# A quantized block of a convolution chain: its depthwise filters on row and column parities in four column strips, with a three-part bfloat16 input

## The chip, the cores and the metric

The kernel runs on one core of a Trainium2 chip. The metric is the device time of one execution in microseconds (us), lower is better; the shown time is the median of three runs. One more execution was profiled: every time below that isn't a run's time comes from its page or its trace.

## The reference, cut to what matters

Four layers follow one another on a tensor of 32 images, 96 channels, 56 x 56. Before each of layers 0, 1, 2 and 3 stands a group norm over groups of three channels of one image, and each layer's result is added to its input. Layer 0 is an inverted bottleneck with squeeze and excite (1x1 to 576 channels, 3x3 depthwise, 1x1 back to 96), layer 1 a three-level wavelet convolution, layer 3 a 9 x 9 depthwise diffusion filter. The change is in layer 2, again an inverted bottleneck, with weights and activations quantized to 4 bits:

```
def quant_w(w, bits):
    t = jnp.tanh(w)
    t = t / (2.0 * jnp.max(jnp.abs(t))) + 0.5
    return 2.0 * quantize_k(t, bits) - 1.0
def act_q(x, bits):
    x = jnp.clip(x, 0.0, 1.0)
    return quantize_k(x, bits)
...
1x1 conv 96 -> 576 (quant_w), bias, batch norm, act_q
3x3 depthwise on 576 (quant_w), bias, batch norm, act_q
1x1 conv 576 -> 96 (quant_w), bias, batch norm
```

The quantized values are integers (weights odd numbers up to 15, activations 0 to 15 after scaling), so bfloat16 holds them exactly. The normalized image is not: it has to go into the first product in more than one part.

## The kernel before, in words

The layers run one after another; between them the tensor goes through device memory (y0, y1, y2). Layers 0 and 2 keep channels on partitions and run over the 32 images; layers 1 and 3 keep rows on partitions and run over channels. An image in layer 2 lies in SBUF as 224 x 14 values: rows in four tiles of 14, columns split by their remainder modulo 4, two images interleaved in a pair (`xt`, three pairs of buffers).

Layer 2 is `layer2` (L987 on), with constants made by `Layer2` (L887 on). Those are prepared in stages beside layer 1's work (`prepare`, L973): tanh, the largest value, quantizing, batch norm factors, and the diagonal matrices of the depthwise filters (`diagonals`, L946: 45 products of 128 x 64). The steps of an image have letters, and `L2_ORDER` (L68) is the order in which every engine issues them: `run_steps` walks the list once for each image n from -2 to 33, a step with "-" belonging to image n-1, "--" to n-2, "+" to n+1. TensorE, VectorE and ScalarE follow this order as written; transfers are issued by SP, powers by GpSimd.

The steps:

- s, u, v, b, x: statistics by `channel_stats` (L91), group mean and variance by small matmuls (L1045, L1053), factors, and the mean taken off the image (L1066).
- h, l: the image times 1/deviation rounded to float32r (`high`, ScalarE, L1079), and what that leaves over (`low`, VectorE, L1085), both written in natural column order, so every fourth element.
- e: `expand` (L1099). Five blocks of 128 channels (the last holds 64 channels twice), four row tiles each: 80 float32r matmuls of 96 x 128 by 392 columns (L1107), a high and a low one into the same PSUM. Each tile is evicted with batch norm and rounding to int16 (`evict`, L1092: ScalarE at L1097, or VectorE at L1095 for those in `L2_ON_DVE`).
- m: `activate`, the clip to 0..15 into a padded bfloat16 tile of pitch 57 (L1116).
- a: `depthwise` (L1129). Nine taps, each a 64 x 64 diagonal matrix; four of them lie side by side in the array (`quarter`, L1121, matmuls at L1126): 648 matmuls of 64 x 64 by 392 columns for an image. A call of a full block fills two PSUM tiles, a call of the half block one; 18 tiles are evicted for an image.
- n: `activate2`, the clip of those (L1116).
- j, d: `project` (L1158), 40 matmuls of 128 x 96 by 392 (L1163), and `add` (L1166), which scales the result and adds it to the image (L1170). In between, r (L1090) has made the image its own residual.
- o: `store` (L1175): statistics for layer 3's norm; after every second image the pair is stored to y2 by six transfers, and the pair's buffer refilled from y1 by six more (`fetch`, L1010).

PSUM has one pool of four tiles of two banks, which all steps share. Layer 0 already does its filters in another way (`filtered`, L417 to L436, and `project`, L474 to L492): in float32, on planes of row and column parities, in strips of 32 array columns. In the trace a float32 matmul is two records.

Of the kernel before, what the change touches and what calls it, by code (L numbers as in the profile page):

```python
# [10 lines left out]
F32 = mybir.dt.float32  # L11
# [26 lines left out]
NM = 12  # L38
MAGIC = 12582912.0
# [29 lines left out]
    e00 e10 e11 e12 l3 j0- d0- e01 e20 e02 e21 r u+ e03 e13 j1- m0 e22 d1- e30 m1 e40 v+ j2- d2- e31  # L69
    e41 e23 b+ e42 j3- x+ e32 e33 m2 d3- m3 s++ e43 h0+ m4 a00 a10 o- a11 n1 a01 a20 h1+ a30 a21 l0+  # L70
    a31 n0 a40 l1+ n2 l2+ a41 n3 n4
"""
L2_ON_DVE = {"e00", "e20", "a301", "a201"}
# [21 lines left out]
def store_norm(tc, S, pool, psum, mv, dram, bias, room=None):  # L95
# [8 lines left out]
    ps = psum.tile([128, 2, 512], F32, tag="mm", name="pn")  # L104
# [79 lines left out]
def layer0(ctx, tc, S, x, w, y0, norm1, tables, aside):  # L184
# [21 lines left out]
    GC = 32  # L206
# [680 lines left out]
class Layer2:  # L887


    def __init__(self, ctx, tc, S, w, y1):  # L890
# [6 lines left out]
        CC, HALF, N9 = NBLK - 1, 64, 2 * NBLK - 1  # L897
        def tile(name, shape, dtype=F32):
            return cp.tile(shape, dtype, tag=name, name=name)

        w1, w2, w3 = (tile(f"{n}q", shape, dtype) for n, shape, dtype in (
            ("l2_w1", [C, NBLK * 128], F32R), ("l2_w2", [128, NBLK, 9], F32), ("l2_w3", [128, N9 + 1, C], BF16)))
        eye2, diag = tile("eye2", [128, HALF]), tile("diag2", [128, NBLK, 9, HALF], BF16)
        mid, out5 = tile("mid2", [128, 10, N9]), tile("out5", [C, 5, 1])
        s1, o1, s2, o2 = (tile(n, [128, N9]) for n in ("s1", "o1", "s2", "o2"))
        s3, o3 = (tile(n, [C, 1]) for n in ("s3", "o3"))
        self.constants = w1, w3, diag, s1, o1, s2, o2, s3, o3

        raw, at = [], 0
        for name, o in (("l2_w1", w1), ("l2_w2", w2), ("l2_w3", w3)):
            p, n = o.shape[0], math.prod(o.shape[1:])
            t = self.pairs[1].rearrange("p r i q -> p (r i q)")[:p, at : at + n]
            m, a = (tile(f"{name}{x}", [p, 1]) for x in "ma")
            raw.append((name, t, o if len(o.shape) == 2 else o.rearrange("p a b -> p (a b)"), m, a))
            at += n

        def load():  # L920
            for name, t, *_ in raw:
                v = w[name]
                nc.sync.dma_start(t, v if len(v.shape) == 2 else v.rearrange("p a b -> p (a b)"))

            nc.sync.dma_start(mid, w["l2_mid"])
            nc.sync.dma_start(eye2, w["eye2"])
            nc.sync.dma_start(out5, w["l2_out"])

        def largest():
            for _, t, _, m, a in raw:  # L930
# [4 lines left out]
        def quantized():  # L935
            for _, t, o, _, a in raw:
# [6 lines left out]
            nc.vector.memset(w3[HALF:, N9 - 1, :], 0.0)  # L943
            nc.vector.memset(w3[:HALF, N9, :], 0.0)

        def diagonals(k):  # L946
            for t in range(9):
                nc.vector.tensor_scalar(diag[:, k, t, :], eye2, w2[:, k, t : t + 1], None, ALU.mult)

        norms = ((mid[:, 0:5, :], s1, o1, 1.0 / 15.0, 15.0), (mid[:, 5:10, :], s2, o2, 1.0 / 225.0, 15.0),  # L950
# [36 lines left out]
def layer2(ctx, tc, S, k2, y1, y2, norm3):  # L987
# [11 lines left out]
    pool = ctx.enter_context(tc.tile_pool(name="l2", bufs=1))  # L999
    sm = ctx.enter_context(tc.tile_pool(name="l2s", bufs=3))  # L1000
    up = ctx.enter_context(tc.tile_pool(name="l2u", bufs=3))
    ap = ctx.enter_context(tc.tile_pool(name="l2a", bufs=6))
    psum = ctx.enter_context(tc.tile_pool(name="l2p", bufs=4, space=PSUM))
    CC, HALF, N9 = NBLK - 1, 64, 2 * NBLK - 1
    w1, w3, diag, s1, o1, s2, o2, s3, o3 = k2.constants
# [17 lines left out]
    apad = padded(cp, nc, NBLK, BF16, "apad")  # L1023
    mv_all = cp.tile([C, B, 2], F32, tag="mv2", name="mv2")
    ims = {}

    def image(b):

        if b not in ims:
            pair, xt = xs.pop(b)  # L1030
            ims[b] = {"b": b, "pair": pair, "xt": xt, "a2": [None] * NBLK, "u": [None] * NBLK, "ps": [None] * NP}
        return ims[b]

# [8 lines left out]
    def group_mean(im):  # L1042
        mean, var = im["mv"][:, 0:1], im["mv"][:, 1:2]
        ps = psum.tile([128, 2, 512], F32, tag="mm", name="pn")
# [6 lines left out]
    def group_variance(im):  # L1051
        ps = psum.tile([128, 2, 512], F32, tag="mm", name="pv")
# [15 lines left out]
    def natural(t, p):  # L1068

        return t.rearrange("c (t r) (q p) -> c p t r q", t=NP, p=NPH)[:, p]  # L1070

    def phase(im, p):
        return im["xt"].rearrange("c (t p r) q -> c p t r q", t=NP, p=NPH)[:, p]

    def high(im, half):
        if half == 0:
            im["hi"] = pool.tile([C, H, W], F32R, tag="hi", name="hi")
        for p in (2 * half, 2 * half + 1):
            nc.scalar.activation(natural(im["hi"], p), phase(im, p), AF.Copy, scale=im["rstd"])  # L1079

    def low(im, i):
        if i == 0:
            im["lo"] = pool.tile([C, H, W], F32R, tag="lo", name="lo")
        for p in range(NPH):
            nc.vector.scalar_tensor_tensor(natural(im["lo"], p)[:, i], phase(im, p)[:, i], im["rstd"],  # L1085
                                           natural(im["hi"], p)[:, i], ALU.mult, ALU.subtract)
# [5 lines left out]
    def evict(out, ps, s, o, c, on_dve):  # L1092

        if on_dve:
# [4 lines left out]
    def expand(im, k, i):  # L1099

        if i == 0:
            im["u"][k] = up.tile([128, HW], I16, tag="u", name="u")
        ps = psum.tile([128, 2, 512], F32, tag="mm", name="ps")
# [390 lines left out]
```

## Time and profile before

| what | time |
|---|---|
| median of 3 runs | 5833.67 us (5833.61 to 5834.31) |
| the profiled execution's own time | 5845.79 us |
| its span in the trace | 5844.0 us |
| layer 2, first statistics to last addition | 3606.6 to 5376.6 us |
| first and last group norm of layer 2 (L1057) | 3612.8 and 5276.1 us |
| first and last expansion matmul (L1107) | 3621.8 and 5337.5 us |
| layer 3, first matmul | 5422.5 us |
| layer 2 from 3622 to 5376 (1754 us): TensorE busy | 1624.0 us |
| VectorE busy in that window | 1208.5 us |
| ScalarE busy in that window | 1212.2 us |
| granted TensorE clock over the span | 0.98 |

A line of a group gives the line of code, the engine, the operation, what it writes and reads, the shape and the count; then busy time and the mean duration of one in ns; then the idle time of the engine before such instructions, and what ended it. "issue" there means that the engine waited for nothing that the profile shows. PEld is TensorE's weight load, which runs beside matmuls. Matmul durations are latencies: successive ones overlap, so a matmul's cost is the distance between starts. A line of the timeline gives start, length, engine, code line, operation and how many were merged. A line of the windows table gives busy time and count for PE, PEld, VectorE, ScalarE and GpSimd, then clock, DMA share and GB/s.

### The profile page before, as it was taken

What the parts mean: (1) busy time and instruction counts of PE and PEld (TensorE: products, weight loads), DVE (VectorE), ACT (ScalarE), POOL (GpSimd) and SP (SyncE); (2) the same over time, 40 slices, a digit from 0 to 9 for tenths busy, and PEclk for the clock granted to TensorE, in tenths of its full rate; (3) what the DMA queues carried; (4) which work ended last, traced back from release to release, by engine and by line L of the source; (5) the groups of instructions that cost most, each with busy time, mean ns of one, the idle gap of its engine ahead of it and who ended that gap; (6) DMA issues with size and microseconds to landing.
All of it is one profiled execution on the core that took longest, in us unless ns stands there. A gap on an engine that the chain in (4) does not pass through costs nothing.

```text
span 5844.0 us, 137224 instructions
## 1 busy us (share of the span) xinstructions
PE 5504.4 (94%) x59688; PEld 3074.4 (53%) x59688; DVE 4693.6 (80%) x5388; ACT 4182.6 (72%) x6036; POOL 240.1 (4%) x156
## 2 busy tenths in 40 slices
PE   5999999999999999995999997999899999897899
PEld 2333333333333333333566665777777777775444
DVE  6999999999999999994766665766667667665777
ACT  5888888888888888874565564766667677675555
POOL 5000000000000000000000000000000000000000
PEclk9999999999999999997999999999999999999999
DMA  3122333332222222235576668386796796754888
GB/s 98 18 56 56 62 60 57 58 58 54 56 49 48 55 52 56 46 26 89 144 141 147 154 147 89 26 44 42 49 46 37 51 49 40 50 31 34 234 253 245
DMA packets 1306412, 454.32 MB, mean 78 GB/s; under 512 B 1123841, under 2 KB 1301753, under 8 KB 1303889
## 3 DMA queue, kind: packets, MB, share of 16 engines
q1 hardware_dynamic: 1305809, 445.54, 50.3%
q8 instruction: 468, 7.67, 0.6%
q14 instruction: 135, 1.11, 0.1%
HBM read 284.44 MB, written 214.08 MB: 85 GB/s over the span
## 4 chain that ended last, share of the span: by engine, by line
PE 83%; ACT 6%; issue 4%; DVE 3%; DMA 2%; POOL 1%; SPq 1%; POOLq 0%; ACTq 0%; DVEq 0%
PE psd L432 17%; PE psd L1126 11%; PE psj L483 10%; PE ps L365 7%; PE pc L842 7%; PE ps L1107 7%; PE pse L388 6%; PE pc L1280 6%; PE psj L1163 3%; ACT hi L1079 2%; PE pc L826 2%; ACT a L1097 2%; PE pa L800 2%; PE pc L816 1%; ACT u L1097 1%
## 5 line engine op out<-in xcount | busy, mean ns | idle before, releaser
L406 DVE SCALAR_TENSOR_TENSOR h<-hpad,l_wdw,h 128x3136 f32<-128x3136 f32 x512 | 1782.2, 3481 | 9.1
L432 PE MATMUL psd<-plane,filt 128*32 128x392 f32 (+5 forms) x16384 | 1084.3, 485 | 0.0
L1126 PE MATMUL psd<-apad,diag 64*64 64x392 bf16 x20736 | 935.9, 333 | 128.1 <-issue 73.0
L1126 PEld LDWEIGHTS <-diag 64*64 64x64 bf16 x20736 | 705.0, 107 | 354.9 <-issue 184.8
L432 PEld LDWEIGHTS psd<-plane,filt 128*32 128x32 f32 (+1 forms) x16384 | 390.1, 108 | 675.2 <-issue 622.7
L1097 ACT ACTIVATE a<-psd,o,s 128x784 int16<-128x784 f32 x448 | 424.1, 999 | 347.8 <-PE psd L1126 347.7
L672 ACT COPY T<-raw 32x112 f32<-32x112 f32 (+2 forms) x1440 | 462.6, 384 | 267.6 <-DMA raw<-tdiff 219.9
L1097 ACT ACTIVATE u<-ps,o,s 128x784 int16<-128x784 f32 x576 | 536.9, 1003 | 160.2 <-PE ps L1107 141.8
L365 PE MATMUL ps<-xn,l_wboth 96*128 96x392 f32 (+1 forms) x1536 | 465.4, 505 | 23.9 <-ACT xn L347 23.0
L406 DVE SCALAR_TENSOR_TENSOR hc<-hhalf,l_wdw,hc 128x1568 f32<-128x1568 f32 x256 | 473.8, 1851 | 16.1 <-ACT hc L399 9.4
L1107 PE MATMUL ps<-hi,l_w1q 96*128 96x392 f32 x1280 | 461.7, 361 | 9.2 <-ACT hi L1079 9.2
L1280 PE MATMUL pc<-x,T 128*112 128x416 f32 (+1 forms) x1152 | 416.2, 524 | 40.3 <-DMA raw<-tdiff 39.6
L842 PE MATMUL pc<-x,T 128*112 128x416 f32 (+1 forms) x1152 | 445.9, 523 | 0.0
L1107 PE MATMUL ps<-lo,l_w1q 96*128 96x392 f32 x1280 | 437.3, 342 | 0.2 <-issue 0.2
L388 PE MATMUL pse<-xn,l_wboth 96*32 96x392 f32 x4096 | 391.2, 500 | 3.2 <-ACT hab L409 3.2
L365 PEld LDWEIGHTS ps<-xn,l_wboth 96*128 96x128 f32 (+1 forms) x1536 | 219.2, 173 | 248.8 <-issue 56.5
L1280 PEld LDWEIGHTS pc<-x,T 128*112 128x112 f32 x1152 | 204.8, 178 | 251.2 <-issue 233.3
L409 ACT ACTIVATE hab<-psd,o,s 128x784 f32<-128x784 f32 x256 | 284.1, 1114 | 58.6 <-PE psd L432 55.8
L375 ACT ACTIVATE hpad<-ps,o,s 128x784 f32<-128x784 f32 x256 | 278.4, 1104 | 49.2 <-PE ps L365 47.9
L483 PE MATMUL psj<-h,wg 128*32 128x392 f32 x3072 | 307.0, 514 | 1.4 <-DVE wg L472 1.4
L483 PE MATMUL psj<-hab,wg 128*32 128x392 f32 x3072 | 304.3, 510 | 0.0
L392 ACT ACTIVATE plane<-pse,o,s 128x784 f32<-128x784 f32 x256 | 256.2, 1001 | 24.9 <-PE pse L388 19.8
(234 smaller groups left out, 7608.2 us busy)
## 6 DMA issues: line engine op xcount, KB each, us to landing
X<-y SPq DMA_DIRECT2D x192, 392.0 KB
y<-xt SPq DMA_DIRECT2D x180, 392.0 KB
xt<-in_x_dram SPq DMA_DIRECT2D x16, 2352.0 KB
y<-y SPq DMA_DIRECT2D x96, 392.0 KB
xt<-y SPq DMA_DIRECT2D x96, 392.0 KB
out_dram<-y SPq DMA_DIRECT2D x96, 392.0 KB
twav<-zwav SPq DMA_DIRECT2D x768, 36.8 KB
raw<-twav SPq DMA_DIRECT2D x96, 168.0 KB
```

What stands on the lines that cost most here:

```text
L365: nc.tensor.matmul(ps[p, j, :NT], wexp[:, k * 128 : k * 128 + 128][:, m], im["xn"][:, j, rows, :].rearrange("c h w -> c (h w)"), start=Tru ...
L388: nc.tensor.matmul(ps[f * GC : (f + 1) * GC, half, :NT].rearrange("p (r w) -> p r w", w=W2), wexp[:, c : c + GC], im["xn"][:, f % 2, r0 : ...
L406: nc.vector.scalar_tensor_tensor(h2, taken(im, k, t), wdw[:, k, t : t + 1], h2, ALU.mult, ALU.add)
L409: nc.scalar.activation(view, ps, AF.Silu, bias=bi[1][:, c : c + 1], scale=sc[1][:, c : c + 1], accum_out=accum)
L432: nc.tensor.matmul(ps[at * GC : (at + 1) * GC, r, :NT].rearrange("p (r w) -> p r w", w=W2)[:, r0 - half * n : r1 - half * n, q0:q1], filt[ ...
L483: nc.tensor.matmul(ps[s * GC : (s + 1) * GC, t, :NT].rearrange("c (m r q) -> c r q m", m=2, q=W4), wg[p, k, c * GC : (c + 1) * GC], phases ...
L672: nc.scalar.copy(to.rearrange("x t (p s) -> x t p s", p=NPH), v[:, k])
L842: nc.tensor.matmul(ps[:PH, to], st["T"][j][:, h, k, :], st["x"][:, j, h, of], start=False, stop=(n == NK - 1))
L1097: nc.scalar.activation(out, ps, AF.Identity, bias=o[:, c : c + 1], scale=s[:, c : c + 1])
L1107: nc.tensor.matmul(ps[:, j, :NT], w1[:, k * 128 : k * 128 + 128], im[part][:, r0 : r0 + RT, :].rearrange("c h w -> c (h w)"), start=(part ...
L1126: nc.tensor.matmul(ps[q, j, :NT].rearrange("p (r w) -> p r w", w=W), diag[p, k, t, :], v, start=(t == 0), stop=(t == 8))
L1280: nc.tensor.matmul(ps[:, :, to], st["T"][:, h, k, :], st["x"][:, h, :, of], start=(n == 0), stop=(n == NK - 1))
```

## The change

In layer 2 alone:

- The image goes into the first product in three bfloat16 parts: `high` rounds to bfloat16 (ScalarE), `remainder` (y) takes the rest in float32 (VectorE), `middle` (i) rounds that (ScalarE), `low` (l) rounds what is left (VectorE). All stay in the image's own layout.
- `expand` works on groups of 32 channels (18 of them): for each group, three parts, two row parities and four strips of 32 array columns, one for each parity of row and column, 24 bfloat16 matmuls. The result lies as four parity planes on four sets of 32 partitions.
- `depthwise` filters these planes with 32-column matrices that gather several taps: a call has 32 matmuls, in four full-height rounds of four and two rounds of eight half-height ones; 18 calls for an image. Border taps shorten the column range, and there is no padding. The filter matrices are made from `l2_wphase` by five products.
- `project` runs in strips of 32 columns (40 matmuls a call, three calls); it puts the columns back in the image's order as it writes PSUM. `add` has four pieces a call.
- All evictions are on ScalarE (`L2_ON_DVE` is empty). PSUM is four named tiles, taken in turn (`bank`). Planes and filtered tiles are fixed sets of buffers (five and six).
- `L2_ORDER` is new; an image now ends ("o") two images behind.

The diff, cut to its core:

```diff
-    e00 e10 e11 e12 l3 j0- d0- e01 e20 e02 e21 r u+ e03 e13 j1- m0 e22 d1- e30 m1 e40 v+ j2- d2- e31
-    e41 e23 b+ e42 j3- x+ e32 e33 m2 d3- m3 s++ e43 h0+ m4 a00 a10 o- a11 n1 a01 a20 h1+ a30 a21 l0+
-    a31 n0 a40 l1+ n2 l2+ a41 n3 n4
+    n4-- s m3-- m4- n0-- a21-- e21- e00- u e32- e02- n2-- a32-- a33-- e01- e13- v e23- a31-- a30-- e30-
+    e22- n1-- n3-- e11- e20- e03- e12- j2-- e33- r- x m2- e31- m1- h j0-- d2-- a40- m0- d0-- a11- y a03-
+    a41- i j1-- d1-- b a23- a20- a00- a10- a22- l a01- a12- e41 e40 o-- a02- e10 a13-
...
-L2_ON_DVE = {"e00", "e20", "a301", "a201"}
+L2_PLANES, L2_ACTS = 5, 6
+L2_ON_DVE = set()
...
         def diagonals(k):
-            for t in range(9):
-                nc.vector.tensor_scalar(diag[:, k, t, :], eye2, w2[:, k, t : t + 1], None, ALU.mult)
+            n = slice(4 * k * NM, min(4 * (k + 1), NGR) * NM)
+            shape = [128, n.stop - n.start, GC]
+            nc.vector.tensor_tensor(filt[:, n, :], eye4.unsqueeze(1).to_broadcast(shape),
+                                    taps[:, n].unsqueeze(2).to_broadcast(shape), ALU.mult)
...
+    def bank(name):
+
+        turn[0] += 1
+        n = turn[0] % 4
+        return psum.tile([128, 2, 512], F32, tag=f"mm{n}", name=name)
...
+    def high(im):
+        nc.scalar.activation(hi, im["xt"], AF.Copy, scale=im["rstd"])
+
+    def remainder(im):
+        nc.vector.scalar_tensor_tensor(rest, im["xt"], im["rstd"], hi, ALU.mult, ALU.subtract)
+
+    def middle(im):
+        nc.scalar.copy(mid, rest)
+
+    def low(im):
+        nc.vector.tensor_tensor(lo, rest, mid, ALU.subtract)
...
+    def expand(im, k, g):
+
+        ps, n = bank("ps"), QUAD * k + g
+        for part in (hi, mid, lo):
+            v = part.rearrange("c (t p r a) q -> c p a t r q", t=NP, p=NPH, a=2)
+            for j in range(2):
+                for f in range(4):
+                    nc.tensor.matmul(
+                        ps[f * GC : (f + 1) * GC, j, :NT].rearrange("p (t r q) -> p t r q", t=NP, q=W4),
+                        w1[:, n * GC : (n + 1) * GC], v[:, f % 2 + 2 * j, f // 2],
+                        start=(part is hi), stop=(part is lo),
+                    )
+        evict(plane(im, k)[:, g, :].bitcast(I16).rearrange("p (m q j) -> p j m q", q=W4, j=2),
+              ps[:, :, :NT].rearrange("p j (m q) -> p j m q", q=W4), s1, o1, n, f"e{k}{g}")
...
+        rounds = [[(r, 2 * r + p, every, 0, 0)] for r in range(2)] + [[(r, 4 + 2 * r + p, every, 0, q)] for r in range(2)]
+        rounds += [[(0, n, bottom, -1, dq), (1, n, top, 1, dq)] for n, dq in ((8 + p, 0), (10 + p, q))]
+        n = HH // 2
+        for x, products in enumerate(rounds):
+            for at, (g, part) in enumerate(parts):
+                for r, m, rows, dm, dq in products:
+                    r0, r1 = max(part * n, -dm), min((part + 1) * n, HH - dm)
+                    q0, q1 = max(0, -dq), W2 - max(0, dq)
+                    nc.tensor.matmul(
+                        ps[at * GC : (at + 1) * GC, r, :NT].rearrange("p (r w) -> p r w", w=W2)[
+                            :, r0 - part * n : r1 - part * n, q0:q1],
+                        filt[rows, (QUAD * k + g) * NM + m, :], planes[rows, g, r0 + dm : r1 + dm, q0 + dq : q1 + dq],
+                        start=(x < 2), stop=(x == len(rounds) - 1),
+                    )
...
+        for t in range(2):
+            for k in range(CC):
+                for s in range(LAST + 1):
+                    strip(s, t, k, slice(128), t * HH, start=(k == 0), stop=False)
+        for s in range(LAST + 1):
+            for t in range(2):
+                strip(s, t, CC, slice(t * HALF, (t + 1) * HALF), 0, start=False, stop=True)
```

In `strip`, the output is written as `ps[...].rearrange("c (m r q) -> c r q m", m=2, q=W4)`, a scatter within PSUM.

## The prediction

> **What bounds the kernel now.** I read the page's busy table and its DMA queues, then the groups by line between 3630 and 5376 us (Layer 2, the only layer whose work the diff changes), then TensorE's weight loads in order of time, then a table of windows over two images.
>
> ```profile
> PE 5504.4 (94%) x59688; PEld 3074.4 (53%) x59688; DVE 4693.6 (80%) x5388; ACT 4182.6 (72%) x6036; POOL 240.1 (4%) x156
> ...
> q8 instruction: 468, 7.67, 0.6%
> ```
>
> Every matmul is a pair of records, a weight load and a matmul. Queue 8 brings instructions: 7.67 MB in 468 packets is 16.4 KB each, and 119,968 TensorE records (592 semaphore ones among them) over 468 is 256. So all of queue 8 is TensorE's program, 256 instructions (64 B each) at a time.
>
> ```profile
> L1126 PE MATMUL psd<-apad,diag 64*64 64x392 bf16 x20736 | 935.9, 333 | 128.1 <-issue 73.0 <-ACT a L1097 52.1 <-ACT u L1097 0.5
> L1107 PE MATMUL ps<-hi,l_w1q 96*128 96x392 f32 x1264 | 454.8, 360 | 0.0
> L1097 ACT ACTIVATE a<-psd,o,s 128x784 int16<-128x784 f32 x448 | 424.1, 999 | 347.8 <-PE psd L1126 347.7
> L1163 PE MATMUL psj<-a,l_w3q 128*96 128x392 bf16 x1024 | 212.1, 329 | 0.0
> ```
>
> TensorE leads: ScalarE waits for it. Its means are latencies; the cost is the distance between starts. In the timeline, L1107 matmuls begin every 0.177 us (4401.65, 4401.83), L1163 every 0.1665, and L1126 runs 288 loads in 12.15 us, 42.2 ns each, 169 ns for four that run side by side. Per image: 80 x 0.1775 = 14.2 us expand, 162 x 0.169 = 27.4 us filter, 40 x 0.1665 = 6.7 us project, 0.5 us statistics: 48.8 us. The first and last group norm lie at 3612.8 and 5276.1: 31 intervals of 53.65 us. Some 4.9 us an image are stalls. Which?
>
> ```profile
> 5293.49 5.25 PEld L1126 LDWEIGHTS <-diag 64*64 64x64 bf16 x128 [2.08 <-issue]
> 5299.70 5.22 PEld L1126 LDWEIGHTS <-diag 64*64 64x64 bf16 x128 [0.96 <-issue]
> 5306.19 5.25 PEld L1126 LDWEIGHTS <-diag 64*64 64x64 bf16 x128 [1.26 <-issue]
> 5312.40 3.70 PEld L1126 LDWEIGHTS <-diag 64*64 64x64 bf16 x92 [0.96 <-issue]
> ```
>
> Bursts of exactly 128 loads, one 256-instruction packet, then a wait for nothing that the profile names. Queue 8's packets start at 5291.03, 5297.31, 5303.73 and 5309.94, always 2.4 to 2.5 us before a burst begins. TensorE is **waiting for its own instructions**. In Layer 2, 59 gaps of over 0.4 us fall on such a border, 92.8 us in all (2.9 us an image); the rest is filter groups waiting for ScalarE to clear PSUM. [...] the packets that were late took a mean 6.39 us while stores run (50 of them), 6.43 while loads run (29) and 3.89 with DMA quiet (13).
>
> ```profile
> 4380.00:4410.00 30.00, 30.00 (x352) 26.63 (x345) 25.17 (x41) 20.70 (x22) 0.55 (x1) 0.99 0.01 2
> 4410.00:4450.00 40.00, 35.75 (x688) 28.51 (x687) 26.66 (x47) 26.87 (x26) 0.00 (x0) 1.00 0.51 59
> 4450.00:4490.00 40.00, 35.80 (x502) 29.92 (x504) 24.73 (x42) 26.34 (x27) 0.54 (x1) 0.96 1.60 65
> ```
>
> The last two columns are the DMA share and GB/s: of each pair of images 30 us are quiet, 40 are stores, 40 are loads. Counted from packets in 1 us steps, 1156 of the 1754 us from 3622 to 5376 have DMA running.
>
> [...] inside Layer 0's L432 the change from 128 to 64 rows takes 411 ns where 309 is usual, so 0.1 us. [...] ScalarE's 784 elements take 1004 ns dense (L392), 1202 at 8 bytes (L347, rows of 14), 1726 at 16 (L1079). [...] L483, which scatters into PSUM, starts a group of four strips every 345 ns, L388 every 330.
>
> **The change, part by part, for one image.**
> *Expand*: three bf16 parts in strips, 18 x 24 = 432 matmuls, 108 groups of four. L388 starts four strips at 7 ns and the next four after 330, the array time of one float32 record; bf16 halves it: 108 x 0.168 = 18.1 us, against 14.2.
> *Filters*: 18 calls of 32 matmuls. L432 does a call (64 records in float32) in 4.19 us (1222.29 to 1226.48). [...] 18 x 1.29 = 23.2 us, against 27.4. [...]
> *Project*: 27 groups at 0.172[...]: 3 x 1.75 = 5.3 us, against 6.7. It scatters into PSUM: bounded by nothing and by a doubling[...]; I take the float32 surplus.
> Sum with statistics: **47.1 us of array, against 48.8**.
> *Instructions*: 432 + 576 + 120 + 4 = 1132 pairs, against 772 (24,704 over 32 in the windows table): 2264 instructions, **8.84 packets where there were 6.03**. At 47.1 us that is 5.33 us a packet, as dense as the bursts above, now all the time.
> *ScalarE*: 36 evictions, back to back 0.92 (1.90 for two, 2.80 for three), 33.1 us[...]. High part and middle part, 3136 elements each, at L399's 2.91: 39 us, from 38. *VectorE*: statistics 8.4, small 1, centre 1.85, remainder 3.5 (L406's 3136), low 3.4, residual 1.9, clips 8.8, twelve adds at 0.58 (L1170) 7.0: 36 us, from 38. Both under TensorE. I let their waits take 5%: 5.6 us a packet.
> *PSUM in turn*: still four tiles of two banks; a filter call takes one, not two. *Border memsets*: 15 on GpSimd, idle for 788 us before; nothing. *Constants*: 45 products of 247 ns become five of some 1.7 (1536 elements at L472's 652 ns for 480, the fixed part taken as 160), and two small loads more, all under Layer 1's matmuls; nothing, and without that cover -2.5 us.
> *Order*: store and refill move from one image behind to two. Both queue on SP as before: 12 transfers for two images, 78 us. From there to the next use by "s" are two iterations, 107 us: covered. The chain "x h y i l" ahead of "e41" is 1.85 + 3 + 3.5 + 2.9 + 3.4 = 15 us; behind "x" stand nine filter calls, three projections and two expansions, some 19 us: covered by 4.
>
> **The sum.** First expand: 3613.4 (the first group norm done) plus that chain, 3628.7, against 3621.8, +7. Packets: 32 x 8.84 = 283. While DMA runs (1156 - 7 = 1149 us; the bytes are the same) a packet takes 6.5, the mean above with a little for unequal latencies: 177. The other 106 at 5.6: 594 us. Draining the last image, whose last filters, clips and projections have no other image beside them: 15. Last matmul at 3628.7 + 1149 + 594 + 15 = 5387, against 5375: +12. Then two more adds, and stores that begin only after the last add (before, from 5371.7 on): +8. Together **+20 us** on the profiled 5845.8 us (span 5844.0), which lies 12 over the median; on the median, **5854**.
>
> **Rivals.**
> *The fetch doesn't bind.* If packets come ahead when the demand is steady, all 283 cost 5.6: 1585 + 15, last matmul at 5229, and 5834 - 146 + 8, **5696**, faster. For it: it needs only a landing within 5.6 us, and quiet stretches show 3.9. Against: 79 late packets under DMA, mean 6.4. Halfway, at 5.9 under DMA: 195 packets and 88 x 5.6, last matmul at 5286, -89 + 8, **5753**. The sign turns near 6.37.
> *PSUM scatter.* If projection doubles, 4.4 us an image: 6.1 us a packet in quiet, and I take half in the rest (6.7): 171 and 112, 1149 + 683 + 15, last matmul at 5476, +101 + 8, **5943**. [...] against: 15 ns in float32.
> *ScalarE binds.* Evictions at L375's 1.10 give 46 us, just under TensorE; quiet packets at 5.9: +32 more, **5886**.
>
> **Chances.** Forecast 0.45 (slower 0.30, same 0.10, faster 0.05, as the sum is flat there); fetch not binding 0.15; halfway 0.12; scatter 0.18; ScalarE 0.10 (0.02 of it same). Faster 0.32, same 0.12, slower 0.56, with 0.2% (12 us) as what a measurement can tell from no change. The range reaches from just under the halfway case to the scatter case: 5745 to 5950; what lies outside is mostly the first rival.
>
> **What would show it.** Queue 8 at some 558 packets (468 + 90). In Layer 2, pauses named "issue" at every 256 TensorE instructions while DMA runs, and few in quiet; pairs per us near 20 in stores and loads, 23 in quiet. Four expand strips every 0.17 us, a filter call near 1.3, ScalarE near 39 us an image. I am wrong if the pauses are at PSUM (scatter, ScalarE) or absent, and if an image takes under 50 us under DMA.

## The result, and the profile after

| | before | after |
|---|---|---|
| median | 5833.64 us (four runs, 5827.23 to 5834.31) | 5907.41 us (four runs, 5899.44 to 5909.51) |
| the profiled execution | 5845.79 us, span 5844.0 | 5899.44 us, span 5897.6 |
| one image of Layer 2, mean distance of group norms | 53.65 us | 54.56 us |
| last projection matmul | 5375.1 us | 5414.8 us |
| Layer 3's first full matmuls | 5422.5 us | 5474.7 us |

The ratio is 1.0126, 95% interval 1.0109 to 1.0144: slower by 74 us, where +20 was forecast. The profiled execution of before lay 12 us above its median and that of after 8 below, so the two traces differ by only 54 us: 40 at the last projection matmul, 12 more until Layer 3 starts.

TensorE's busy line and the instruction queue, from the page of the changed kernel:

```profile
PE 5571.7 (94%) x71208; PEld 2670.0 (45%) x71208; DVE 4579.4 (78%) x4899; ACT 4501.2 (76%) x6036; POOL 260.7 (4%) x141
...
q8 instruction: 558, 9.14, 0.7%
```

11,520 pairs more are 90 packets more: 558, as forecast. The groups by line in Layer 2 (3630 to 5415 us):

```profile
L1151 PE MATMUL psd<-plane,filt 128*32 128x392 bf16 (+5 forms) x16384 | 673.1, 331 | 38.3 <-issue 35.0 <-ACT act L1112 2.5 <-ACT acth L1112 0.6
L1112 ACT ACTIVATE act<-psd,o,s 128x784 int16<-128x784 f32 x512 | 632.5, 1250 | 76.1 <-PE psd L1151 72.4 <-ACT act L1112 0.3
L1112 ACT ACTIVATE plane<-ps,o,s 128x784 int16<-128x784 f32 x512 | 601.6, 1249 | 141.3 <-PE ps L1121 136.6 <-ACT act L1112 0.2 <-PE pv L1076 0.2
...
L1169 PE MATMUL psj<-act,l_w3q 128*32 128x392 bf16 x3072 | 281.2, 526 | 5.3 <-issue 2.3 <-ACT plane L1112 1.7 <-DVE act L1131 1.2
```

TensorE hardly waits for ScalarE now: 2.5 us ahead of the filters, where it was 52. What is left is "issue". Two things are off the forecast: an eviction lasts 1.25 us where the kernel before has 1.00 (back to back, as the forecast counted, a median 1.15 where it put 0.92), and a projection matmul lasts 526 ns where the other matmuls last 331 to 338. How the waits named "issue" lie is seen in the weight loads in order of time, during stores:

```profile
4462.13 0.45 PEld L1151 LDWEIGHTS <-filt 128*32 128x32 bf16 x14 [1.42 <-issue]
4462.90 0.14 PEld L1151 LDWEIGHTS <-filt 64*32 64x32 bf16 x16 [0.33 <-issue]
4463.36 0.45 PEld L1151 LDWEIGHTS <-filt 128*32 128x32 bf16 x16 [0.32 <-issue]
4464.14 0.14 PEld L1151 LDWEIGHTS <-filt 64*32 64x32 bf16 x16 [0.33 <-issue]
4464.60 2.74 PEld L1121 LDWEIGHTS <-l_w1q 96*32 96x32 bf16 x66 [0.32 <-issue]
4468.89 3.13 PEld L1121 LDWEIGHTS <-l_w1q 96*32 96x32 bf16 x77 [1.56 <-issue]
```

14 + 16 + 16 + 16 + 66 loads are 128, one packet of 256 instructions, with 1.42 us of waiting ahead of it and 1.56 after it. The 0.3 us ahead of the other rows recur at every change between 128 and 64 rows, at no packet's border. The table of windows, for a quiet stretch, a store and a load (the columns are those of the prediction's table):

```profile
4402.00:4430.00 28.00, 27.49 (x550) 15.96 (x542) 16.58 (x17) 24.08 (x20) 1.15 (x1) 1.00 0.01 3
4432.00:4472.00 40.00, 35.73 (x803) 19.97 (x804) 22.81 (x38) 33.67 (x29) 1.15 (x1) 0.96 0.54 62
4474.00:4510.00 36.00, 33.84 (x701) 15.36 (x696) 26.92 (x40) 27.95 (x22) 0.00 (x0) 0.95 1.71 64
```

Pairs per us: 20.1 in the store and 19.5 in the load, as forecast (20), but 19.6 in quiet, where 23 were forecast. The quiet stretch is what is wrong.

To compare kernels below I count TensorE's records in steps of 1 us, by whether DMA runs in the step, and divide by 256: us per packet. Kernel after, 3624 to 5370 us: 6.42 under DMA (174.5 packets), **6.14 in quiet** (102). The forecast had 6.5 (177) and 5.6 (106).

### The profile page after: what moved, and what is told of

It reads as the page before. It is cut to its first block, busy times and chain, and to the rows that moved or that the text cites. A ratio compares the mean times of both kernels' runs of the same rounds, so it can differ in the third digit from the quotient of the medians.

```text
span 5897.6 us, 159737 instructions
## 1 busy us (share of the span) xinstructions
PE 5571.7 (94%) x71208; PEld 2670.0 (45%) x71208; DVE 4579.4 (78%) x4899; ACT 4501.2 (76%) x6036; POOL 260.7 (4%) x141
## 4 chain that ended last, share of the span: by engine, by line
PE 88%; DMA 4%; DVE 3%; issue 2%; ACT 1%; SPq 1%; POOL 1%; ACTq 0%; DVEq 0%; POOLq 0%
PE psd L434 17%; PE psd L1151 12%; PE ps L1121 11%; PE psj L485 10%; PE ps L367 7%; PE pc L844 7%; PE pse L390 6%; PE psj L1169 5%; PE pc L1300 3%; PE pc L828 2%; DMA raw<-tdiff 2%; PE pa L802 2%; PE pc L818 1%; DMA X<-y 1%; PE pc L842 1%
## 5 line engine op out<-in xcount | busy, mean ns | idle before, releaser
L1112 ACT ACTIVATE plane<-ps,o,s 128x784 int16<-128x784 f32 x512 | 601.6, 1249 | 141.3 <-PE ps L1121 136.6
L1151 PE MATMUL psd<-plane,filt 128*32 128x392 bf16 (+5 forms) x16384 | 673.1, 331 | 38.3 <-issue 35.0
L1112 ACT ACTIVATE act<-psd,o,s 128x784 int16<-128x784 f32 x512 | 632.5, 1250 | 76.1 <-PE psd L1151 72.4
L1121 PEld LDWEIGHTS <-l_w1q 96*32 96x32 bf16 x13824 | 448.4, 95 | 243.0 <-issue 143.8
L1151 PEld LDWEIGHTS <-filt 128*32 128x32 bf16 (+1 forms) x18432 | 312.1, 92 | 453.1 <-issue 390.0
L1121 PE MATMUL ps<-lo,l_w1q 96*32 96x392 bf16 x4608 | 356.3, 337 | 15.9 <-issue 13.1
L1121 PE MATMUL ps<-mid,l_w1q 96*32 96x392 bf16 x4608 | 346.9, 336 | 24.2 <-issue 18.6
L1186 DVE SCALAR_TENSOR_TENSOR xt<-psj,s,xt 32x392 f32<-32x392 f32 (+1 forms) x384 | 223.8, 621 | 177.1 <-PE psj L1169 175.4
L1121 PE MATMUL ps<-hi,l_w1q 96*32 96x392 bf16 x4608 | 339.9, 338 | 21.0 <-issue 13.1
```

What stands on the lines that cost most here:

```text
L1112: nc.scalar.activation(out, ps, AF.Identity, bias=o[:, c : c + 1], scale=s[:, c : c + 1])
L1121: nc.tensor.matmul(ps[f * GC : (f + 1) * GC, j, :NT].rearrange("p (t r q) -> p t r q", t=NP, q=W4), w1[:, n * GC : (n + 1) * GC], v[:, f % ...
L1151: nc.tensor.matmul(ps[at * GC : (at + 1) * GC, r, :NT].rearrange("p (r w) -> p r w", w=W2)[:, r0 - part * n : r1 - part * n, q0:q1], filt[ ...
```

## The experiments

Theory at the start: a projection call takes 3.2 us, not 1.75, because it scatters into PSUM. Rivals: ScalarE's evictions (1.25 us) hold the kernel back; or instruction fetch under DMA makes the whole difference.

**e1: dense PSUM.** The moving operand is read in the order in which PSUM lies.

```diff
-                ps[...].rearrange("c (m r q) -> c r q m", m=2, q=W4),
-                ... v.rearrange("p r (q j m) -> p j r q m", j=2, m=2)[:, n % 2], **ends)
+                ps[...].rearrange("c (m r q) -> c m r q", m=2, q=W4),
+                ... v.rearrange("p r (q j m) -> p j m r q", j=2, m=2)[:, n % 2], **ends)
```

> The changed kernel with the projection reading its columns in the order (m, r, q), so that it writes PSUM densely; same work. Scatter theory: a projection call falls from 3.2 us to near 1.75 (4.4 us of array an image, 139 in all); late instruction packets take part of it back while DMA runs, so 60 to 100 us faster than the changed kernel (some 5810 to 5850). ScalarE theory (its evictions of 1.25 us set the pace): 0 to 20 us. If scatter costs nothing: no change, and the call stays at 3.2 us.

Measured: 5926.05 us, ratio 1.0155 (1.0132 to 1.0178), slower than the changed kernel, and a call takes 3.4 us. The call did not shorten. I took this for proof that the scatter is harmless and blamed the reading. That was a mistake of the experiment, not only of the theory: the edit changed two things, as it also turned a reading of pairs of values into one of single values, 8 bytes apart. e6 and e10 part the two.

**e2: dense evictions.** Planes are written in order, and filtered rows as two halves, one for each column parity. The projection then reads single values 56 bytes apart and still scatters.

```diff
-        evict(plane(im, k)[:, g, :].bitcast(I16).rearrange("p (m q j) -> p j m q", q=W4, j=2),
-              ps[:, :, :NT].rearrange("p j (m q) -> p j m q", q=W4), s1, o1, n, f"e{k}{g}")
+        evict(plane(im, k)[:, g, :].bitcast(I16).rearrange("p (n j) -> p n j", j=2),
+              ps[:, :, :NT].rearrange("p j n -> p n j"), s1, o1, n, f"e{k}{g}")
...
-        ... .rearrange("c (m r) (q p) -> c p r m q", r=2, p=2)[:, p],
+        ... .rearrange("c (m r) (p q) -> c p r m q", r=2, p=2)[:, p],
...
-                ... v.rearrange("p r (q j m) -> p j r q m", j=2, m=2)[:, n % 2], **ends)
+                ... v.rearrange("p r (m q j) -> p j r q m", j=2, m=2)[:, n % 2], **ends)
```

> The changed kernel with dense eviction writes: planes written in order with PSUM read across its two banks, filtered rows kept as two column parities side by side; the projection still scatters. Both theories: evictions fall from 1.25 us to about 1.0. TensorE and packets set the pace: 5 to 35 us faster (gaps that are on no packet border sum to 65 us, the drain of the last image 4). ScalarE sets it: over 100 us faster (36 x 0.25 us x 32 = 288).

Measured: evictions at 1.00 us in place of 1.25, and 5948.15 us, ratio 1.0192 (1.0177 to 1.0207): slower than the changed kernel. A projection call takes 3.6, which is 1.1 us of array an image more, so the edit is not clean. But nine us an image less of ScalarE, against 1.1 more of the array, would have made the kernel faster if ScalarE set the pace: it is not the bound. e8 shows it without that flaw.

**e3 and e4: both kernels without Layer 2's stores and refills.**

```diff
-            if b >= 2 * len(k2.pairs):
+            if 2 * len(k2.pairs) <= b < 6:
...
-        store_images(nc, y2, im)
...
-        layer3(tc, w, y2, norm3, td, out)
+        layer3(tc, w, y1, norm3, td, out)
```

> The changed kernel without layer 2's stores and refills: it goes over the same six image buffers again and again, and layer 3 reads layer 1's result; that part of the computation is left out. Late-packet theory: the gaps on borders of 256 TensorE instructions (110, 116 us) all but vanish, the distance between group norms falls from 54.6 us to 51 or 52, packets land within some 4 us. If the gaps have another cause: the distance stays within 1 us of 54.6.

> The kernel before with the same left out (layer 2's stores and refills; layer 3 reads layer 1's result). Late-packet theory: its 59 border gaps (93 us) vanish, the distance between group norms falls from 53.65 us to 50.5 or 51. So with DMA away the changed kernel still loses 0.5 to 1.5 us an image: that part isn't the fetch but the array (50.8 against 48.8 us). If the fetch made the whole difference, the changed kernel is the faster of the two here.

Measured: 5744.8 us for the changed kernel, 5660.76 for the kernel before; at most nine waits at packet borders are left (6 us and 2 us in all). The powers of the group norms on GpSimd, once an image, first of e3, then of e4:

```profile
4414.39 1.14 POOL L1080 TENSOR_TENSOR rstd<-ve,mhalf 96x1 f32<-96x1 f32 x1 [50.46 <-DVE ve L1078]
4466.01 1.15 POOL L1080 TENSOR_TENSOR rstd<-ve,mhalf 96x1 f32<-96x1 f32 x1 [50.48 <-DVE ve L1078]
```

```profile
4381.89 0.55 POOL L1057 TENSOR_TENSOR rstd<-ve,mhalf 96x1 f32<-96x1 f32 x1 [48.94 <-DVE ve L1055]
4431.42 0.55 POOL L1057 TENSOR_TENSOR rstd<-ve,mhalf 96x1 f32<-96x1 f32 x1 [48.98 <-DVE ve L1055]
```

51.6 us an image against 49.5 once the rows are steady (over all 31 intervals, a short first one among them, 50.74 and 48.66). So the changed kernel is the slower one with hardly an instruction late: more packets cannot be the whole cause. The distance is larger without DMA (84 us, one run of each) than with it (54 between the traces, 74 between the medians).

**e5: neighbours in, dense out.** The filtered tile is stored by column phase, each eviction cut in two for it; a strip then reads two runs of 196 values and writes PSUM in order.

```diff
+        for j in range(2):
+            evict(u.rearrange("c (j p m r q) -> c j p r m q", j=2, p=2, r=2, q=W4)[:, j, p],
+                  ps[:, :, :NT].rearrange("c r (m q j) -> c j r m q", q=W4, j=2)[:, j], s2, o2, k, f"a{k}{i}")
...
-                ps[...].rearrange("c (m r q) -> c r q m", m=2, q=W4),
-                ... v.rearrange("p r (q j m) -> p j r q m", j=2, m=2)[:, n % 2], **ends)
+                ps[...].rearrange("c (m x) -> c m x", m=2),
+                ... v[:, n % 2, :, n // 2 * 196 : (n // 2 + 1) * 196], **ends)
```

> The changed kernel with the filtered tile stored by column phase: each eviction of the filters is cut in two (392 elements each), and every strip of the projection then reads two runs of 196 neighbouring bfloat16 values and writes PSUM densely. The result is that of the reference. Theory READ (the strips' short-run reading of SBUF is what makes a projection call 3.2 us instead of the forecast 1.75): the call falls to about 1.75, 4.4 us an image; in quiet stretches, where the array sets the pace (5.88 us a packet), 109 packets times 0.49 us come back, and under DMA some 174 times 0.26 if a packet still needs 6.5: about 100 us less than the changed kernel's 5907, some 5808, below the kernel before. Theory FETCH (instructions set the pace nearly everywhere): the call falls, but the time only by some 50, 5857. Theory MODE (the strips or the half-row products are slow whatever they read): the call stays at 3.2 and the time near 5907. Eighteen of 36 evictions become two of some 0.6 us: ScalarE about the same.

Measured: **5838.87 us, ratio 1.0002** (0.9986 to 1.0017); a call takes 1.73 to 1.8 us. The slowdown is gone: 68 us less than the changed kernel's median. Its windows, quiet, store and load:

```profile
4379.00:4409.00 30.00, 30.00 (x714) 18.88 (x706) 18.50 (x21) 28.51 (x32) 1.14 (x1) 1.00 0.01 4
4411.00:4451.00 40.00, 35.26 (x789) 20.36 (x787) 22.31 (x33) 34.23 (x44) 1.15 (x1) 0.96 0.54 62
4451.00:4481.00 30.00, 24.87 (x578) 11.39 (x569) 25.37 (x38) 23.79 (x29) 0.00 (x0) 1.00 1.71 67
```

Quiet rose from 19.6 to 23.8 pairs per us; store (19.7) and load (19.3) did not move. Over Layer 2, 5.44 us a packet in quiet in place of 6.14, and 6.51 under DMA in place of 6.42. The shorter call is worth 0.70 us for each of some 105 quiet packets, 73 us; under DMA the array now waits longer at the borders (170 us there, 112 in the changed kernel). This is the fetch expectation's pattern (it said 50 us); that of the reading theory (100 us) counted on a gain under DMA that didn't come.

Waiting seems to have a second price here, which the forecast did not count. The last image of e5, and the windows table from 5346.2 to 5356.2 us:

```profile
5347.68 0.51 PE L1151 MATMUL psd<-plane,filt 64*32 64x351 bf16 x2 [4.44 <-issue]
...
5352.75 2.81 PE L1171 MATMUL psj<-act,l_w3q 128*32 128x392 bf16 x32
5355.49 0.53 PE L1171 MATMUL psj<-acth,l_w3q 64*32 64x392 bf16 x8
5355.94 1.69 PE L1171 MATMUL psj<-act,l_w3q 128*32 128x392 bf16 x32
```

```profile
5346.20:5356.20 10.00, 7.28 (x86) 2.74 (x89) 3.42 (x6) 1.25 (x2) 0.00 (x0) 0.50 1.31 35
```

After a pause of 4.44 us the granted clock is 0.50, and a call takes 3.19 us (5355.94 - 5352.75) with nothing scattered. Between 3640 and 5360 us the traces show 34 us at that clock for the kernel before, 20 for the changed one, 61 for e5, 85 for e11 and 55 for e12, in stretches of 3.4 to 10.2 us; each began 1.5 to 5.4 us after the start of a pause of TensorE of at least 1.3 us. At a clock of 0.50 at most half of such a stretch is lost: as an estimate from the 61 and 20 us, up to 20 us more in e5 than in the changed kernel. How much of it the waiting for packets hides, no run shows.

**e6: which half of it.** The three calls of an image made unlike.

```diff
+            if i < 2:
+                v = v.rearrange("p r w -> p (r w)")[:, n % 2 * NT : (n % 2 + 1) * NT]
+            else:
+                v = v.rearrange("p r (q j m) -> p j r q m", j=2, m=2)[:, n % 2]
...
+            if i != 1:
+                o = o.rearrange("c (m r q) -> c r q m", m=2, q=W4)
```

> The changed kernel with its three projection calls of an image made unlike: the first reads 392 neighbouring values but still scatters into PSUM, the second reads neighbours and writes PSUM densely, the third is left as it is. Calls one and two leave the columns out of order, so part of the projection is not the reference's. Theory READ: calls one and two take about 1.75 us, call three 3.2. Theory SCATTER (refuted once already, as a dense PSUM with an even shorter reading run gave 3.4): one and three 3.2, two 1.75. Theory MODE: all three 3.2.

Its matmuls in order of time, calls one (neighbours in, scatter) and two (neighbours in, dense), each with the row that follows:

```profile
3754.53 2.89 PE L1178 MATMUL psj<-act,l_w3q 128*32 128x392 bf16 x32
3757.35 0.52 PE L1178 MATMUL psj<-acth,l_w3q 64*32 64x392 bf16 x8
3757.80 1.30 PE L1151 MATMUL psd<-planeh,filt 128*32 128x392 bf16 x32
...
3762.74 1.51 PE L1178 MATMUL psj<-act,l_w3q 128*32 128x392 bf16 x32
3764.18 0.36 PE L1178 MATMUL psj<-acth,l_w3q 64*32 64x392 bf16 x8
3764.47 1.31 PE L1151 MATMUL psd<-plane,filt 128*32 128x392 bf16 x32
```

3757.80 - 3754.53 = 3.27 us with neighbours read but PSUM scattered; 1.73 with both in order. My reading theory falls, and the scatter, which e1 seemed to have cleared, is the cause after all. A group of four strips takes (3757.35 - 3754.53) / 8 = 353 ns.

**e7: the scatter alone, in the kernel before.** Its four calls in the full 128 x 96 form: as it is, reading pairs, scattering, both.

```diff
+                if i % 2:
+                    v = im["a2"][k][:, (n - j) * NT : (n - j + 2) * NT].rearrange(
+                        "p (r q b m) -> p b r q m", q=W4, b=2, m=2)[:, j]
...
+                if i >= 2:
+                    o = o.rearrange("c (m r q) -> c r q m", m=2, q=W4)
```

> The kernel before with the four projection calls of an image made unlike, in its full 128 x 96 form: the first as it is (neighbouring values in, dense PSUM out), the second reads runs of two values, 8 bytes apart, the third reads neighbours and scatters into PSUM as the changed kernel does, the fourth does both. Calls two to four leave the columns out of order, so part of the projection is not the reference's. A call is ten matmuls, 1.67 us as it is. If a short-run read costs every matmul by itself, calls two and four take about 3.2; if it costs only where four strips read four streams at once, all four take 1.67, and the cost belongs to the strips and the read together. If the scatter costs, calls three and four are longer than one and two.

Medians of a call: 1.52, 1.59, **3.01, 2.99** us. One of the two that scatter, and the expansion after it:

```profile
4382.96 1.48 PE L1173 MATMUL psj<-a,l_w3q 128*96 128x392 bf16 x4
4384.24 0.53 PE L1173 MATMUL psj<-a2c,l_w3q 128*96 128x392 bf16 x1
4384.57 1.52 PE L1173 MATMUL psj<-a,l_w3q 128*96 128x392 bf16 x4
4385.88 0.53 PE L1173 MATMUL psj<-a2c,l_w3q 128*96 128x392 bf16 x1
4385.95 0.64 PE L1107 MATMUL ps<-hi,l_w1q 96*128 96x392 f32 x1
```

The step from one matmul to the next is 0.33 us (4384.24 to 4384.57) where it is 0.1665 in order. So the price belongs to the write, not to strips: two scattered calls of four cost 3.0 us an image, 95 over 32 images. The single run took 5928.94 us, 94 above the median of the runs beside it; between the traces, first group norm to last projection is 73 us longer than in the kernel before. So most of the cost, perhaps all of it, passed into the time.

**e8: dense expansion evictions on top of e5** (the first hunk of e2).

> As the kernel with the filtered tile stored by column phase, and the expansion's evictions written densely as well (ScalarE's 18 from 1.25 to 1.00 us, 4.5 us an image). If TensorE's array and its instructions alone set the pace, it takes the same time as that kernel, about 5808 (within 10). If ScalarE's evictions have become the bound once the projection is short, it is faster by up to 4.5 us an image where they bind: down to some 5700.

Measured: 5837.77 us, ratio 1.0005 (0.9991 to 1.0019). Those evictions fall from 1255 to 1005 ns, and nothing is gained: ScalarE does not bind here either.

**e9: e5 without Layer 2's DMA** (the edits of e3).

> The changed kernel with the filtered tile stored by column phase (dense reading and writing in the projection), and without Layer 2's stores and refills: six images of y1 are used over and over and Layer 3 reads y1, so the output is not the reference's. Without DMA instructions come in time, and the distance between group norms shows the array alone: 51.5 us an image for the changed kernel, 49.36 for the kernel before. Theory SCATTER+FETCH (the projection's writing cost 4.35 us an image; what is left between the forecast array sum of 47.1 and the 52.8 with DMA is instruction fetch): 47.2 us an image, a total near 5607. Rival SCALARE (evictions cap the rate once the projection is short, which could also be why the dense expansion evictions gave nothing under DMA): 49 to 50 us, a total near 5690.

```profile
4445.97 1.14 POOL L1080 TENSOR_TENSOR rstd<-ve,mhalf 96x1 f32<-96x1 f32 x1 [46.06 <-ACT plane L1112]
4493.14 1.15 POOL L1080 TENSOR_TENSOR rstd<-ve,mhalf 96x1 f32<-96x1 f32 x1 [46.02 <-ACT plane L1112]
```

47.17 us an image, and 5605.95 us in all; 47.2 and 5607 were expected. The array sum of the forecast, 47.1, is right for this kernel, if by two small errors that cancel: from the mean distances between starts here (43.5, 39.0 and 45.1 ns), expansions take 18.8 us where 18.1 stood, filters 22.5 where 23.2 stood, projections 5.4 where 5.3 stood. With instructions in time it beats the kernel before by 2.3 us an image. What DMA costs has to be taken over the same 31 intervals: e5 goes from 46.65 to 52.84, 6.2 us an image, and the kernel before from 48.66 to 53.65, 5.0. Of e5's 192 us over these intervals some 170 are the waits at packet borders.

**e10: reading.** All three calls in strips: pairs of values 8 bytes apart, into dense PSUM; single values 8 bytes apart, into dense PSUM; neighbours, into runs of 14 in PSUM.

```diff
+            if i == 0:
+                v = v.rearrange("p r (q j m) -> p j r q m", j=2, m=2)[:, n % 2]
+                o = o.rearrange("c (r q m) -> c r q m", q=W4, m=2)
+            elif i == 1:
+                v = v.rearrange("p r (q j m) -> p j m r q", j=2, m=2)[:, n % 2]
+                o = o.rearrange("c (m r q) -> c m r q", m=2, q=W4)
...
+                o = o.rearrange("c (r m q) -> c m r q", m=2, q=W4)
```

> The changed kernel with its three projection calls of an image made unlike, all in strips: the first keeps its reading (runs of two values, 8 bytes apart) and writes PSUM densely, the second reads single values 8 bytes apart and writes densely (the form that took 3.4 us a call before), the third reads neighbours and writes PSUM in runs of 14. All leave columns out of order, so the projection is not the reference's. Known: neighbours and dense 1.73, neighbours and the changed kernel's scatter 3.27. If only the writing costs and single-value reading is a second cost of its own: 1.8, 3.4, and 1.8 if runs of 14 are long enough in PSUM. If any reading of short runs costs in strips: 3.2, 3.4 and 1.8. If every PSUM write out of order costs, call three takes 3.2.

Calls one and two in order of time:

```profile
3749.18 1.66 PE L1180 MATMUL psj<-act,l_w3q 128*32 128x392 bf16 x32
3750.78 0.37 PE L1180 MATMUL psj<-acth,l_w3q 64*32 64x392 bf16 x8
3751.07 1.30 PE L1151 MATMUL psd<-planeh,filt 128*32 128x392 bf16 x32
...
3756.01 3.01 PE L1180 MATMUL psj<-act,l_w3q 128*32 128x392 bf16 x32
3758.95 0.53 PE L1180 MATMUL psj<-acth,l_w3q 64*32 64x392 bf16 x8
3759.41 0.85 PE L1151 MATMUL psd<-plane,filt 128*32 128x392 bf16 x16
```

1.89 us for pairs, 3.40 for single values; the third took 1.97, and the call at that place takes 1.96 in e5. So runs of 14 cost nothing in PSUM, and reading single values is a second cost of the same size, which e1 put in the place of the first.

**e11: fewer instructions.** e5 with the projection in its full form, four calls of ten matmuls.

```diff
+        for t in range(2):
+            for k in range(NBLK):
+                p, r0 = (slice(128), t * HH) if k < CC else (slice(t * HALF, (t + 1) * HALF), 0)
...
+                nc.tensor.matmul(
+                    ps[:C, t, :NT].rearrange("c (m x) -> c m x", m=2), w3[p, k, :],
+                    v[:, i % 2, :, i // 2 * 196 : (i // 2 + 1) * 196], start=(k == 0), stop=(k == CC))
```

> The changed kernel with the filtered tile stored by column phase, and the projection in its full form again: 128 x 96, four calls of ten matmuls (1.52 us each) in place of three of 40 in strips (1.73), eight additions an image in place of twelve. The result is the reference's. Array work grows by 0.9 us an image, the instruction pairs fall by 80 of 1132: 8.2 packets an image in place of 8.84, some 538 on queue 8. Theory FETCH (under DMA a packet takes 6.5 us and sets the pace): under DMA 53.4 us an image in place of 57.5, in quiet 48 in place of 47.1; over Layer 2 some 60 us less than the kernel with strips (5839): about 5775. Theory ARRAY: 0.9 us an image more, about 5865.

Measured: 5909.53 us, ratio 1.0137 (1.0106 to 1.0167), 538 packets. Neither theory. A call takes 2.18 us, not 1.52, which is 2.6 us of array work an image that I had not counted. Two suspects: the two matmuls of 64 rows among those of 128, and the change from strips to the full form and back. Of the 71 us above e5, up to 12 are the half clock (85 us of it, where e5 has 61).

**e12: the same with all matmuls on 128 rows**, zeros in the weights of the unwanted half.

```diff
+    w3z = cp.tile([128, 2, C], BF16, tag="w3z", name="w3z")
...
-                p, r0 = (slice(128), t * HH) if k < CC else (slice(t * HALF, (t + 1) * HALF), 0)
+                r0, wt = (t * HH, w3[:, k, :]) if k < CC else (0, w3z[:, t, :])
```

> As the full-form projection, whose ten matmuls took 2.18 us a call in place of 1.52 because two of the ten had 64 rows between matmuls of 128; here those two take all 128 rows, with zeros in the weights for the half that is not wanted, and nothing else is changed. The result is the reference's. A call should take 1.52 us, so the array work is 46.9 + 0.7 = 47.6 us an image (2.6 less), and the packets stay 8.2 an image. Theory FETCH: under DMA 6.5 us a packet, 53.4 us an image; in quiet 5.9 us a packet, 48.4 an image: some 22 images pass in 1177 us of DMA and ten in the rest, together about 60 us less than the strips with dense writing (5839), near 5780, which is below both kernels; against the full form with 64-row matmuls (5909) some 130 less, although only 84 us of array work go. Theory ARRAY (the number of instructions does not matter, only the array sum): 0.7 us an image more than the strips, near 5860.

Measured: 5853.77 us, ratio 1.0039 (1.0022 to 1.0055): 15 us above e5, not 60 below. A call takes 1.79 us: of the 0.66 us, the row changes were 0.39, and the rest stays, with the change of form as what is left to explain it; no run tests that alone. Over 3650 to 5300 us, waits at packet borders under DMA fall from 170 us in e5 (122 of them) to 106 (82): fewer instructions did help. But in quiet the instructions around cost more as well (22.0 ns for one of the expansion where e5 has 20.8, 21.0 and 20.5 for the filters, 89.7 and 23.8 for the projection's 80 and 240): 1.0 + 0.5 + 1.5 = 3.0 us more array work an image. The two nearly cancel. No kernel tried here beats the kernel before by more than its measurement can tell.

## Why the prediction was right, and where its size was wrong

**The main limit: as forecast.** 558 packets; under DMA 174.5 packets at 6.42 us where 177 at 6.5 stood; pauses at each 256 instructions (1.42 and 1.56 us around the packet shown above); and without DMA (e9, with the projection as the forecast had priced it) the array sum of 47.1 us to within 0.1. That the array work could be cut by 4.4 us an image without moving the store and load stretches (e5) is the clearest sign that packets set the pace there. The forecast's times of late packets (6.39, 6.43 and 3.89 us) count from a moment of request that it assumed and no row shows; the 6.42 rests on counts alone. Its 1.29 us for a filter call was an estimate too; 32 starts at 39.0 ns (e9) make 1.25.

**That it came out slower: in part luck.** The forecast's +20 us rested on packets alone, with a projection of 1.75 us. e5 is nearly that kernel (its filter evictions are cut in two besides), and it is not measurably slower: ratio 1.0002, 0.9986 to 1.0017. Late instructions ate the gain that e9 shows over e4 (55 us, one run of each); they did not turn it into a loss. What made the changed kernel slower than the kernel before is the scatter, which the forecast had as a rival.

**The step that failed: "*Project*: 27 groups at 0.172 ... I take the float32 surplus".** The forecast read Layer 0's scattered groups (345 ns against 330) as a surcharge of 15 ns. The runs fit a floor instead: a group that scatters takes about 0.35 us in both types (345 ns in float32, 353 in bfloat16 in e6). In float32 a group in order takes 330 ns, nearly as long, and the floor hardly shows; in bfloat16 it takes 180 (e6's dense call, (3764.18 - 3762.74) / 8). The forecast's 1.75 us a call are nine groups at 0.172 and two changes of row count at the 0.1 us of L432. The doubling that stood there as the other bound, 4.4 us an image, was the truth: 3 x (3.2 - 1.75) = 4.35.

**The rival that named it was priced too high.** Its 5943 let packets under DMA take 6.7 us. They took 6.42: the longer call filled time in which TensorE would have waited for its instructions (112 us of waits at borders under DMA, 170 in e5). The cost shows in quiet alone, 106 x (6.14 - 5.6) = +57 us, with -14 under DMA (177 x -0.08). The last matmul came at 5415 in place of 5387, 28 later; the remaining -15 lie in start and drain, which I did not separate. With the scatter gone (e5) the time is 5838.9, 15 below the forecast; its quiet packets took 5.44 us where 5.6 stood, which is worth 17.

**ScalarE: wrong size, no effect.** The sum of 39 us an image took evictions at 0.92 back to back; at 1.15 ScalarE is busy for 48 us (1532 us from 3622 to 5440, over 32 images). The forecast had taken a stride of 4 bytes as free, an estimate that no row showed; its own 1202 ns at 8 bytes against 1004 dense was a fifth more already. 48 us is over the rival's input (46 us), but its outcome, a bound, is refuted by e2 and e8.

**The tail: 12 us, for 8.** From the last projection to Layer 3's first full matmuls 47.4 us before, 59.9 after, 60.8 in e5. It takes back most of what e5 had won: its last projection comes 17.5 us before that of the kernel before, its Layer 3 only 4. No run takes the tail apart.

**Mean packets: a weakness that the forecast got away with.** It compared a mean array time of a packet with the time of a packet under DMA. If a packet that takes longer than that saves nothing for the next, which no row shows directly, the comparison has to be made packet by packet. As an estimate from measured times: take each packet's array time from its lines' quiet durations, and under DMA the larger of that and 6.45 us (the changed kernel took 6.42, e5 6.51).

| 3650 to 5300 us (after, e11: to 5370, 5360; before: to 5330) | sum by packet | sum by mean | measured |
|---|---|---|---|
| before | 1628 | 1520 | 1688 |
| after | 1762 | 1741 | 1724 |
| e5 | 1652 | 1652 | 1649 |
| e11 | 1720 | 1663 | 1716 |
| e12 | 1666 | 1629 | 1652 |

In e5 every packet is alike (5.42 us, deviation 0.24), so the mean serves. Before, packets of filters (128 loads in 5.25 us) alternate with packets of expansions of over 10 us, whose surplus, in this estimate, repays nothing. That would be how the kernel before lost 5.0 us an image though its mean packet (8.2 us) is longer than 6.45, why most of e7's scatter showed in its time, and why e11 and e12 were forecast too fast. The estimate is 3.6% short for the kernel before and 2% long for the changed one: it comes nearer than the mean for three kernels, ties for e5 and is further off for the changed one. It fits, and is not proof.

**Open:** why a packet takes some 6.4 us while DMA runs, and how far ahead it is asked for; what the half clock after pauses costs; and whether fewer instructions with the same array work would have won, which no kernel here isolates.

## What to carry to other kernels

A surcharge read off a slow data type may be a floor that the type hides, as here: compare absolute times per group, not differences, before carrying it to a type whose group takes about half the time (180 ns here, for 330). Where two limits alternate (here instruction fetch while transfers run, 6.42 to 6.51 us a packet, and the array otherwise, 5.44 to 6.14), price a saving stretch by stretch: the shorter projection was worth 0.70 us a packet in quiet and nothing under DMA. And an experiment that undoes one access pattern must not bring in another: e1 exchanged a scattered write for a single-value read, and its null result misled me until e6.

## What the runs showed of the hardware

- Writing PSUM one float32 value at a time, alternating between places 784 bytes apart, took 0.33 us for 392 columns in the full form (e7, 0.1665 in order) and 0.353 us a group in strips (e6), 3.27 us a call against 1.73 in order. Runs of 14 took the same time as dense writing (e10: 1.97 us a call, 1.96 in e5).
- Reading bfloat16 moving data in pairs, 8 bytes apart, cost almost nothing (1.59 against 1.52 us in the full form, e7; 1.89 in e10 against 1.73 to 1.8 in strips); single values 8 bytes apart nearly doubled the call in strips (3.40, e10).
- ScalarE's int16 writes at a stride of 4 bytes took 1250 ns for 784 elements (the changed kernel), dense ones 1003 (e2).
- TensorE's instructions came in packets of 256: 468 packets for 119,968 records before, 90 packets more for 11,520 pairs more. While the stores and refills ran, a kernel of short matmuls took 6.4 to 6.5 us a packet, whether a packet took 5.44 us in quiet (e5: 6.51 under DMA) or 6.14 (the changed kernel: 6.42).
- The 54 stretches of half clock counted under e5 all followed pauses of TensorE of 1.3 us or more; with no DMA beside Layer 2 there was none between 3680 and 5150 us (e9).
